# A graph-attention layer on one core: five growing chunks of edges in two shared DRAM tables, instead of four chunks with a table each

## The chip, the cores and the metric

The kernel runs on one core of a Trainium2 chip. The metric is the time of one execution on the device in microseconds; the times before the change come from 16 runs. One execution was also taken with the hardware profiler; durations in this document come from that one. The engines are TensorE (PE, with its weight loads as PEld), VectorE (DVE), ScalarE (ACT), GpSimd (POOL) and SyncE (SP), which here only issues DMAs.

## The reference: what is computed

A graph with 12,500 nodes of 128 features and 412,500 edges of 64 features, sorted by `dst`. With h = relu(layernorm(x)):

```python
q, k, v = h @ Wq + bq, h @ Wk + bk, h @ Wv + bv
eh = edge_features @ We + be
attn_in = concatenate([q[src], k[dst], eh], axis=-1)          # per edge, 3 x 128
hmid = leaky_relu(attn_in @ A1 + b1, 0.2)                      # per edge, 128
scores = leaky_relu(hmid @ A2 + b2, 0.2)                       # per edge, 8 heads
w = softmax(scores.mean(axis=-1), axis=0)                      # over all edges
out = segment_sum(w[:, None] * v[dst], src, num_segments=N)
y = h @ Wn + bn + out
return x + gamma * layernorm(y) + beta
```

The softmax runs over all edges at once, values are gathered at `dst`, and the sum goes to `src`. So the edges come sorted by one end and are needed by the other.

## The kernel before, in words

**Blocks and tiles.** The nodes are padded to 12,544 and split into 98 blocks of 128: node n is in block n mod 98, at place n // 98 (`place1` holds the place plus one). Edges come in 3,224 tiles of 128, eight tiles to a group (`SUPER`), 403 groups.

**Chunks.** `CHUNKS` cuts the groups into four: 86, 121, 121 and 75 groups. For each chunk a table in DRAM, `tabs[c]`, has for each of the 98 blocks room for `ct` tiles of edges: the mean number of a chunk's edges per block plus 3.75 of its roots, rounded up to tiles. That makes 8, 11, 11 and 7 tiles a block. Behind these rows lies a region of `OTHER` tiles for edges that found no room; those are dealt with by a slow loop at the end (`other_edges`), which doesn't run when there are none. A row has 257 numbers (`ROW`): the place, 128 numbers of the part of the hidden layer that comes from `dst` and the edge, and 128 of the value.

**First stage** (`first_stage(c)`): for each tile of edges two matmuls in one PSUM bank (L679 edge features times folded weights, L682 a window of node rows picked by a selection matrix), moved out by ACT (L662 the place, L665 the rest) into `row`, of which there are seven buffers, each for two tiles; then GpSimd scatters each tile of rows to its slots in the table by an indirect DMA (L621).

**Getting ready** (`ready(c)`): `count` makes a histogram of the chunk's edges by block and lane group; `plan` (L397) turns it into starting slots, and into `trips`, the number of turns of `clear_rest`; `place_slots` (L436) works out each edge's slot by matmuls that add up ranks (L459) and comparisons and maxima on DVE (L452, L503).

**Zeroing.** A slot that no edge took must hold numbers, and its place must be 0, since `scores` (L779) tells free slots by place 0 and gives them -1e30. `clear_ends(c)` zeroes the last two tiles (`SPARE`) of each block's room, 98 DMAs of 257 KB a chunk on SP's queue. `clear_rest(c)` zeroes the tiles before these in a loop, if any block has so few edges that it doesn't reach them.

**Second stage** (`second_stage`): for each block of a chunk SP loads its rows (`load`, L699, six buffers), the places are turned (L709), written to DRAM and spread over the partitions (`put_places` L716, `spread_places` L722, both on SP's queue). Tiles go in quads (`QUAD` is 4): `turn` transposes them on PE (L738) and adds the query part by three matmuls (L741), `steep` applies the leaky rectifier (L749 on ACT, L750 on DVE). Then, once for a block and through one PSUM tile `s_ps`: `heads_of` (L758), `add_bias` (L765), `leaky` (L769), `by_slot` (L775), `scores` (L783 to L789), `turn_top` (L792), `top_of_all` (L796), `spread_top` (L799), `exponentials` (L805 to L810). Last, for each tile, weights on DVE (L824) and the product with the values on PE (L833), added to `acc` (L838). A plan (`at(when, ...)`) puts these jobs into steps, two per quad; the single-tile chain through `s_ps` takes five steps, and the products of a block come `LAG` = 11 steps after its first turn.

**Order.** The last loop (L982) runs c from 0 to the number of chunks: stage c has the first stage of chunk c, the second stage of chunk c - 1, the getting ready of chunk c + 1 and its `clear_ends`. `interleave` mixes their steps in proportion, and PE, DVE, ACT and SP keep the order that is written out (`manual_schedule`), so on each of these engines an instruction that waits holds up all behind it. `clear_rest(c)` stands ahead of each stage; also when it makes no turn, SP waits there for DMAs that it issued. Before the loop, the node tables (`nodes`), the first part of `ready(0)` and `clear_ends(0)` run together. After it come `all_sums` and the writing out of the nodes.

Of the kernel before, what the change touches and what calls it, by code (L numbers as in the profile page):

```python
# [10 lines left out]
FP = mybir.dt.float32  # L11
# [5 lines left out]
ALU = mybir.AluOpType  # L17
AX = mybir.AxisListType
# [4 lines left out]
P = 128  # L23
# [6 lines left out]
SUPER = 8  # L30
# [7 lines left out]

SPARE = 2

OTHER = 960

STR = 5

# [2 lines left out]
ROW = 2 * D + 1  # L47
# [2 lines left out]
MAGIC = float(3 << 22)  # L50

NGRP = 5
CHUNKS = (0.213, 0.3, 0.3, 0.187)
BECAUSE = "worked out within these bounds on the chip"


# [46 lines left out]
def kernel(ctx: ExitStack, tc: tile.TileContext, n_edges, x, src, dst, ea, w_nv, w_qt, w_kt,  # L103
# [12 lines left out]
    nc = tc.nc  # L116
    NP = x.shape[0]
    NTN = NP // P
    NT = src.shape[1]
    NG = NT // SUPER  # L120
    NBIN = DIG * DIG
# [3 lines left out]
    chunks = []  # L125
    g0 = 0
    for i, share in enumerate(CHUNKS):
        n = NG - g0 if i == len(CHUNKS) - 1 else max(1, round(NG * share))
# [4 lines left out]
    NC = len(chunks)  # L133
    most_tiles = max(ct for _, _, ct, _ in chunks)

    blocks = []
# [15 lines left out]
    flag_d = dram.tile([P, NT], FP, name="flag_d")  # L152
    hist_d = dram.tile([STR, DIG, DIG], FP, name="hist_d")

    tabs = [dram.tile([(t + min(n * SUPER, OTHER)) * P, ROW], FP, name=f"tab{c}") for c, (_, n, _, t) in enumerate(chunks)]

    late = ctx.enter_context(tc.tile_pool(name="late", bufs=1))
    blank = late.tile([P, SPARE * ROW], FP, name="blank")
# [2 lines left out]
    def clear_ends(c):  # L161

        ct = chunks[c][2]
        k = min(SPARE, ct)
        for b in range(NTN):
            nc.sync.dma_start(out=tabs[c][(b * ct + ct - k) * P:(b + 1) * ct * P, :].rearrange("(p j) r -> p (j r)", p=P),
                             in_=blank[:, 0:k * ROW])
            yield


# [28 lines left out]
    bins_b = const.tile([P, NBIN], BF, name="bins_b")  # L199
    nc.vector.tensor_copy(bins_b, bins_f)  # L200
    edge_f = iota("edge_f", 8 * STR, 0, P, 1)

    part1 = iota("part1", 1, 1, 0, 1)
    third = const.tile([P, 1], FP, name="third")
# [155 lines left out]


    start_of = {}

    def count(c):

# [31 lines left out]
    def plan(c):  # L397

        ct = chunks[c][2]
        whole = ip.tile([1, STR, NBIN], FP, name="whole_h")  # L400
        nc.sync.dma_start(out=whole[:, :STR, :], in_=hist_d.rearrange("s a b -> s (a b)").unsqueeze(0))
        yield
        start_of[c] = ip.tile([1, STR * NBIN], FP, name="start_of")
        so = start_of[c].rearrange("p (s b) -> p s b", s=STR)
        nc.vector.memset(so[:, 0, :], 0.0)
        for s in range(1, STR):
            nc.vector.tensor_add(so[:, s, :], so[:, s - 1, :], whole[:, s - 1, :])

        least = ip.tile([1, 2], FP, name="least")
        total = whole[:, STR - 1, :]  # L410
        nc.vector.tensor_add(total, so[:, STR - 1, :], whole[:, STR - 1, :])

        nc.vector.tensor_reduce(least[:, 1:2], total, AX.X, ALU.max)
        nc.vector.tensor_scalar(least[:, 1:2], least[:, 1:2], MARK, 1e6, op0=ALU.is_ge, op1=ALU.mult)
        nc.vector.tensor_scalar(start_of[c], start_of[c], least[:, 1:2], None, op0=ALU.add)
        nc.vector.tensor_reduce(least[:, 0:1], total[:, 0:NTN], AX.X, ALU.min)
        nc.vector.tensor_scalar(trips[:, c:c + 1], least[:, 0:1], float((ct - min(SPARE, ct)) * P), float(NTN),
                                op0=ALU.is_lt, op1=ALU.mult)
        yield

    def clear_rest(c):

        ct = chunks[c][2]
        rest = ct - min(SPARE, ct)
        if rest > 0:
            turns = nc.values_load(trips[0:1, c:c + 1], min_val=0, max_val=NTN, skip_runtime_bounds_check_because=BECAUSE)
            with tc.For_i(0, turns, 1) as b:
                for j in range(rest):
                    nc.sync.dma_start(out=tabs[c][ds(b * (ct * P) + j * P, P), :], in_=blank[:, 0:ROW])

    def values(row, engine, high):

# [182 lines left out]
    def scatter(c, g, k, row, sent):  # L615

        g0 = chunks[c][0]
        m = min(P, n_edges - (g * SUPER + k) * P)
        if m > 0:
            t = (g - g0) * SUPER + k  # L620
            i = nc.gpsimd.indirect_dma_start(  # L621
                out=tabs[c][:, :], out_offset=bass.IndirectOffsetOnAxis(ap=slots[c][t // (8 * STR)][:m, t % (8 * STR):t % (8 * STR) + 1], axis=0),
                in_=row[:m, :], in_offset=None)

            for other in sent[-OTHER + 1:]:
                tc.declare_no_dep(i.ins, other, reason="every edge has a slot of its own")
            sent.append(i.ins)
# [64 lines left out]
    def second_stage():  # L692
# [6 lines left out]
        def load(i):  # L699
            c, b, ct, _, _ = blocks[i]  # L700
            rows_of[i] = pb.tile([P, most_tiles, ROW], FP, name="rows_of")
            nc.sync.dma_start(out=rows_of[i][:, 0:ct, :],
                              in_=tabs[c][b * ct * P:(b + 1) * ct * P, :].rearrange("(p j) r -> p j r", p=P))
            qws[i] = ps.tile([P, 3 * D], BF, name="qw")
            nc.sync.dma_start(out=qws[i], in_=q_tab[b])

# [71 lines left out]

        def scores(i):  # L779

            _, b, ct, _, _ = blocks[i]
            none = ps.tile([P, most_tiles], FP, name="none")[:, 0:ct]
            nc.vector.tensor_scalar(none, rows_of[i][:, 0:ct, 0:1].rearrange("p j r -> p (j r)"), 0.0, -1e30,  # L783
                                    op0=ALU.is_equal, op1=ALU.mult)
            state["score", i] = score = ps.tile([P, most_tiles + 1], FP, name="score")
            nc.vector.tensor_copy(score[:, ct:ct + 1], most_of[:, b:b + 1])
            nc.vector.tensor_add(score[:, 0:ct], state["s_ps"][:, 0:ct], none)
# [276 lines left out]
```

## Time and profile before

| | |
|---|---|
| median of 16 runs | 6141.63 us (6125.76 to 6165.45) |
| the profiled execution | 6131.44 us, span 6129.7 us |
| busy: PE, DVE, POOL, ACT | 4973.3, 4535.7, 3382.2, 2204.1 us |
| mean granted clock of TensorE | 0.915 |
| moved by DMA | 1362.10 MB, 222 GB/s over the span |
| first scatter; stages 1, 2, 3 begin (first scatter of their chunk); last scatter ends | 470.1; 1404.8, 2724.8, 4136.1; 5220.8 us |
| last addition to `acc` ends | 5987.1 us |

The lines are read like this: a group's line has the source line, engine, operation, what it writes from what, the count, then busy us, mean ns of one, and the idle time just before them with what ended it. Matmuls overlap in these records, so that groups add up to more than the busy time of their engine. A stage is judged by the windows between the times above, not by the shares over the whole span: the first stage of the loop has no attention in it, and the last has no scatter.

### The profile page before, as it was taken

What the parts mean: (1) busy time and instruction counts of PE and PEld (TensorE: products, weight loads), DVE (VectorE), ACT (ScalarE), POOL (GpSimd) and SP (SyncE); (2) the same over time, 40 slices, a digit from 0 to 9 for tenths busy, and PEclk for the clock granted to TensorE, in tenths of its full rate; (3) what the DMA queues carried; (4) which work ended last, traced back from release to release, by engine and by line L of the source; (5) the groups of instructions that cost most, each with busy time, mean ns of one, the idle gap of its engine ahead of it and who ended that gap; (6) DMA issues with size and microseconds to landing.
All of it is one profiled execution on the core that took longest, in us unless ns stands there. A gap on an engine that the chain in (4) does not pass through costs nothing. (4 is left out here: it accounts for less than half of the span.)

```text
span 6129.7 us, 98826 instructions
## 1 busy us (share of the span) xinstructions
PE 4973.3 (81%) x31430; PEld 3421.5 (56%) x31788; DVE 4535.7 (74%) x14001; ACT 2204.1 (36%) x5624; POOL 3382.2 (55%) x3236
## 2 busy tenths in 40 slices
PE   1556676658988999879998989979999999888880
PEld 0223343335666666656666666657777777656550
DVE  4886686657877777768777777767777777777779
ACT  0452222223444444434444444434444444333331
POOL 0007777777777777767777777765555565000000
PEclk9777767778999999989999999989999999999995
DMA  9345555557888888877888988877888878444443
GB/s 202 119 158 176 169 164 171 171 162 244 259 253 261 259 259 262 256 225 257 276 279 274 284 274 271 276 238 255 261 261 264 260 265 258 154 151 150 156 129 126
DMA packets 607897, 1362.10 MB, mean 222 GB/s; under 512 B 120436, under 2 KB 337196, under 8 KB 569352
## 3 DMA queue, kind: packets, MB, share of 16 engines
q1 hardware_dynamic: 423284, 877.57, 48.8%
q0 software_dynamic: 154704, 424.26, 19.3%
q10 hardware_dynamic: 29380, 53.87, 2.6%
q8 instruction: 252, 4.13, 0.3%
q14 instruction: 277, 2.27, 0.1%
HBM read 782.14 MB, written 573.14 MB: 221 GB/s over the span
## 5 line engine op out<-in xcount | busy, mean ns | idle before, releaser
L621 POOL DMA_INDIRECT tab<-row,slots x3223 | 3380.4, 1049 | 1820.3 <-issue 720.1
L679 PE MATMUL row_ps<-w_ea,ea_t 128*128 128x256 f32 x3224 | 1103.3, 427 | 292.5 <-ACT row L665 255.4
L833 PE MATMUL o_ps<-rows_of,w 128*128 128x128 f32 x7252 | 1087.1, 293 | 12.6 <-DVE w L824 11.7
L665 ACT ACTIVATE row<-row_ps 128x512 f32<-128x512 f32 x1612 | 944.2, 586 | 415.9 <-PE row_ps L682 392.8
L824 DVE TENSOR_SCALAR w<-iota_f,rows_of,score 128x128 f32<-128x128 f32 x3626 | 1025.5, 353 | 6.3
L750 DVE TENSOR_TENSOR rows_of<-h_ps,low 128x512 f32<-128x512 f32 (+1 forms) x980 | 634.3, 647 | 469.4 <-ACT low L749 466.3
L679 PEld LDWEIGHTS row_ps<-w_ea,ea_t 128*128 128x128 f32 x3224 | 600.4, 209 | 649.8 <-ACT row L665 430.7
L833 PEld LDWEIGHTS o_ps<-rows_of,w 128*128 128x128 f32 x7252 | 918.7, 196 | 43.0 <-DVE w L824 23.8
L749 ACT ACTIVATE low<-h_ps 128x512 f32<-128x512 f32 (+1 forms) x980 | 552.0, 563 | 860.8 <-PE h_ps L741 856.3
L741 PE MATMUL h_ps<-sel_q,qw 128*128 128x512 bf16 (+1 forms) x2582 | 719.8, 365 | 52.5 <-DVE sel_q L729 32.2
L682 PE MATMUL row_ps<-kv,sel 126*128 126x256 bf16 x3224 | 668.2, 291 | 18.2 <-DMA offs<-off_d 15.7
L662 ACT ACTIVATE row<-place 128x2 f32<-128x2 bf16 x1612 | 318.7, 198 | 997.4 <-DMA tab<-row,slots 971.3
L503 DVE TENSOR_REDUCE num<-run 128x5 f32<-128x500 f32 x646 | 433.3, 671 | 297.5 <-PE run L459 297.3
L738 PE MATMUL h_ps<-ident,rows_of 128*128 128x128 f32 x3626 | 574.0, 278 | 0.0
L775 PEld LDWEIGHTS s_ps<-heads,z 96*128 96x128 f32 (+1 forms) x3136 | 392.7, 194 | 206.2 <-DVE z L769 191.1
L682 PEld LDWEIGHTS <-sel 126*128 126x128 bf16 x3224 | 338.8, 105 | 299.6 <-issue 76.5
L758 PE MATMUL s_ps<-rows_of,a_sb 128*32 128x512 f32 (+1 forms) x1960 | 454.2, 579 | 55.8 <-DVE most_of L805 31.6
L738 PEld LDWEIGHTS h_ps<-ident,rows_of 128*128 128x128 f32 x3626 | 436.1, 144 | 107.9 <-issue 81.7
L775 PE MATMUL s_ps<-heads,z 96*128 96x3 f32 (+1 forms) x3136 | 415.2, 253 | 88.2 <-DVE z L769 87.5
L765 ACT ACTIVATE z<-s_ps,b_col 64x512 f32<-64x512 f32 (+1 forms) x392 | 266.7, 680 | 512.9 <-PE s_ps L758 512.1
L452 DVE TENSOR_TENSOR one<-bins_b,block 128x500 f16<-128x500 bf16 x646 | 431.3, 668 | 1.7 <-PE run L459 1.6
L729 DVE TENSOR_SCALAR sel_q<-pls,part 128x1408 bf16<-128x1408 uint8 (+2 forms) x392 | 333.2, 850 | 116.9 <-DMA pls<-pl_d 107.7
(172 smaller groups left out, 4725.9 us busy)
## 6 DMA issues: line engine op xcount, KB each, us to landing
rows_of<-tab SPq DMA_DIRECT2D x196, 1413.5 KB
ea_t<-in_ea SPq DMA_DIRECT2D x403, 256.0 KB
tab<-blank SPq DMA_DIRECT2D x392, 257.0 KB
rows_of<-tab SPq DMA_DIRECT2D x98, 1028.0 KB
rows_of<-tab SPq DMA_DIRECT2D x98, 899.5 KB
tab<-row,slots POOLq DMA_INDIRECT x3223
offs<-off_d SPq DMA_DIRECT2D x403, 126.0 KB
qw<-q_tab SPq DMA_DIRECT2D x392, 96.0 KB
```

What stands on the lines that cost most here:

```text
L621: i = nc.gpsimd.indirect_dma_start(out=tabs[c][:, :], out_offset=bass.IndirectOffsetOnAxis(ap=slots[c][t // (8 * STR)][:m, t % (8 * STR):t ...
L665: nc.scalar.activation(row[:, :, 1:ROW], bank, AF.Copy)
L679: nc.tensor.matmul(bank[:, :, 0:D], lhsT=ea_g[:, ts(k, P)], rhs=w_ea, start=True, stop=False, skip_group_check=True)
L682: nc.tensor.matmul(bank[:, b, :], lhsT=sel[:, ts(b * halves + k, P)], rhs=kv, start=False, stop=True, skip_group_check=True)
L738: nc.tensor.matmul(h_ps[:, ts(j, P)], lhsT=rows_of[i][:, q * QUAD + j, 1:D + 1], rhs=ident, is_transpose=True, start=j == 0, stop=False, s ...
L741: nc.tensor.matmul(h_ps[:, 0:m * P], lhsT=qws[i][:, ts(k, D)], rhs=plss[i][:, q * QUAD * P:(q * QUAD + m) * P], start=False, stop=k == 2, ...
L749: nc.scalar.activation(low, h_ps, AF.Copy, scale=SLOPE)
L750: nc.vector.tensor_max(rows_of[i][:, q * QUAD:q * QUAD + m, 1:D + 1], h_ps.rearrange("p (j e) -> p j e", j=m), low.rearrange("p (j e) -> p ...
L758: nc.tensor.matmul(state["s_ps"][32 * q:32 * (q + 1), 0:m * P], lhsT=a2_sb, rhs=rows_of[i][:, q * QUAD:q * QUAD + m, 1:D + 1], start=True, ...
L775: nc.tensor.matmul(state["s_ps"][:, 0:nq * QUAD].rearrange("p (q j) -> p j q", j=QUAD)[:, j, :], lhsT=state["z"][:32 * nq, ts(j, P)], rhs= ...
L824: nc.vector.tensor_scalar(w, iota_f, rows_of[i][:, t, 0:1], state["score", i][:, t:t + 1], op0=ALU.is_equal, op1=ALU.mult)
L833: nc.tensor.matmul(state["o_ps"][:, 0:D], lhsT=w, rhs=rows_of[i][:, t, D + 1:ROW], start=t == 0, stop=t == ct - 1)
```

## The change

The edges are cut into five chunks of 50, 62, 86, 109 and 96 groups. Chunk c uses table c mod 2, so that chunks 0, 2 and 4 share one table and 1 and 3 the other. `held[c]` is the number of tiles that earlier chunks filled in the same table; the ends of a chunk's blocks are zeroed only where they lie behind that, and `clear_rest` and its test are limited to those blocks too. Since what lies in a free slot may now be an old edge's row with a place of its own, free slots are no longer told by place 0: `plan` spreads each block's number of edges over the partitions (`taken[c]`), and `scores` compares slot numbers (`slot_of`) with it. `OTHER` goes from 960 to 840.

```diff
-OTHER = 960
+OTHER = 840
-CHUNKS = (0.213, 0.3, 0.3, 0.187)
+CHUNKS = (0.124, 0.154, 0.2135, 0.2705, 0.238)
...
-    tabs = [dram.tile([(t + min(n * SUPER, OTHER)) * P, ROW], FP, name=f"tab{c}") for c, (_, n, _, t) in enumerate(chunks)]
+    tiles_of = [max(t + min(n * SUPER, OTHER) for _, n, _, t in chunks[i::2]) for i in range(2)]
+    tabs = [dram.tile([t * P, ROW], FP, name=f"tab{i}") for i, t in enumerate(tiles_of)]
+
+    held = [max([t for _, _, _, t in chunks[c % 2:c:2]], default=0) for c in range(NC)]
...
         for b in range(NTN):
-            nc.sync.dma_start(out=tabs[c][(b * ct + ct - k) * P:(b + 1) * ct * P, :].rearrange("(p j) r -> p (j r)", p=P),
-                             in_=blank[:, 0:k * ROW])
+            if (b + 1) * ct > held[c]:
+                nc.sync.dma_start(out=tabs[c % 2][(b * ct + ct - k) * P:(b + 1) * ct * P, :]
+                                  .rearrange("(p j) r -> p (j r)", p=P), in_=blank[:, 0:k * ROW])
             yield
...
+    slot_of = {ct: iota(f"slot{ct}", ct, 0, 1, ct) for ct in sorted({ct for _, _, ct, _ in chunks})}
...
-        nc.vector.tensor_reduce(least[:, 0:1], total[:, 0:NTN], AX.X, ALU.min)
-        nc.vector.tensor_scalar(trips[:, c:c + 1], least[:, 0:1], float((ct - min(SPARE, ct)) * P), float(NTN),
+        b0 = min(held[c] // ct, NTN - 1)
+        nc.vector.tensor_reduce(least[:, 0:1], total[:, b0:NTN], AX.X, ALU.min)
+
+        nc.vector.tensor_scalar(total, total, least[:, 1:2], None, op0=ALU.subtract)
+        run = ps_c.tile([P, 512], FP, name="run")
+        nc.tensor.matmul(run[:, 0:NBIN], lhsT=ones[0:1, :], rhs=total, start=True, stop=True)
+        taken[c] = late.tile([P, NBIN], FP, name=f"taken{c}")
+        nc.vector.tensor_copy(taken[c], run[:, 0:NBIN])
+        nc.vector.tensor_scalar(trips[:, c:c + 1], least[:, 0:1], float((ct - min(SPARE, ct)) * P), float(NTN - b0),
                                 op0=ALU.is_lt, op1=ALU.mult)
...
-        if rest > 0:
-            turns = nc.values_load(trips[0:1, c:c + 1], min_val=0, max_val=NTN, skip_runtime_bounds_check_because=BECAUSE)
+        b0 = held[c] // ct
+        if rest > 0 and b0 < NTN:
+            turns = nc.values_load(trips[0:1, c:c + 1], min_val=0, max_val=NTN - b0, skip_runtime_bounds_check_because=BECAUSE)
             with tc.For_i(0, turns, 1) as b:
                 for j in range(rest):
-                    nc.sync.dma_start(out=tabs[c][ds(b * (ct * P) + j * P, P), :], in_=blank[:, 0:ROW])
+                    nc.sync.dma_start(out=tabs[c % 2][ds(b * (ct * P) + (b0 * ct + j) * P, P), :], in_=blank[:, 0:ROW])
...
         def scores(i):
 
-            _, b, ct, _, _ = blocks[i]
+            c, b, ct, _, _ = blocks[i]
             none = ps.tile([P, most_tiles], FP, name="none")[:, 0:ct]
-            nc.vector.tensor_scalar(none, rows_of[i][:, 0:ct, 0:1].rearrange("p j r -> p (j r)"), 0.0, -1e30,
-                                    op0=ALU.is_equal, op1=ALU.mult)
+            nc.vector.tensor_scalar(none, slot_of[ct], taken[c][:, b:b + 1], -1e30, op0=ALU.is_ge, op1=ALU.mult)
```

The scatter and the loads of the second stage take `tabs[c % 2]` for `tabs[c]`; all else is as before. In both kernels every block's edges fit its room, and every block fills all but its last two tiles: neither `clear_rest` nor `other_edges` makes a turn on this input.

## The prediction

> **What bounds the kernel now.** I read first the page's 40 slices, then the busy time by stage (windows cut where the scatter of a new chunk starts), then the waits of the stage in which one half of the work stands alone, and last the windows around a stage's start. "Stage k" is the pass of the last loop in which chunk k is built; the chunk before it is consumed in the same stage.
>
> The page: busy tenths of TensorE, VectorE and GpSimd, then the granted clock.
>
> ```profile
> span 6129.7 us, 98826 instructions
> PE   1556676658988999879998989979999999888880
> ...
> DVE  4886686657877777768777777767777777777779
> ...
> POOL 0007777777777777767777777765555565000000
> PEclk9777767778999999989999999989999999999995
> ```
>
> TensorE is full from slice 10 on, but not before: there GpSimd alone is steady, and in the last slices GpSimd has nothing left. By stage (columns: window, its length, then busy us of PE, weight loads, DVE, ACT, POOL with instruction counts, clock, DMA share, GB/s):
>
> ```profile
> 470.00:1405.00 935.00, 631.81 (x3092) 348.06 (x3091) 607.87 (x1690) 240.98 (x697) 711.66 (x689) 0.76 0.52 168
> 1405.00:2725.00 1320.00, 1166.45 (x7421) 814.87 (x7525) 997.03 (x3215) 531.08 (x1437) 999.21 (x969) 0.94 0.84 256
> 2725.00:4136.00 1411.00, 1275.74 (x8532) 934.72 (x8637) 1052.99 (x3325) 578.88 (x1554) 1026.14 (x968) 0.96 0.85 269
> 4136.00:5222.00 1086.00, 1043.05 (x7030) 772.70 (x7127) 816.12 (x2644) 453.37 (x1191) 643.41 (x599) 1.00 0.80 259
> 5222.00:5987.00 765.00, 668.82 (x4294) 458.04 (x4343) 588.96 (x2130) 233.65 (x500) 0.00 (x0) 1.00 0.45 147
> 5987.00:6130.00 143.00, 0.59 (x2) 0.50 (x2) 134.89 (x223) 19.95 (x41) 0.00 (x0) 0.51 0.41 135
> ```
>
> Stage 0 and stage 1 are GpSimd's: the timeline shows each scatter busy 0.96 to 1.5 us and then 0.30 us of issue, and 935 us / 688 is 1.359 us a scatter; in stage 1, 1307 us / 968 is 1.351. The page has the scatter as its dearest row:
>
> ```profile
> L621 POOL DMA_INDIRECT tab<-row,slots x3223 | 3380.4, 1049 | 1820.3 <-issue 720.1
> ```
>
> In stage 2 GpSimd and TensorE are both nearly full and neither is quite; stage 3 is TensorE's (1043 of 1086 us). In stage 4 attention runs alone, 7.47 us a block, and TensorE waits in it for one chain through one PSUM tile (the waits of PE in that stage: total us, times, longest):
>
> ```profile
> PE s_ps L799 <- DVE top_of L796: 58.0, 94, 0.7
> PE s_ps L775 <- DVE z L769: 26.7, 94, 1.5
> ```
>
> That is 0.9 us a block: heads, bias, leaky, turn, maximum, spread follow one another through PE, ACT and DVE, whatever number of tiles the block has.
>
> **What the work costs.** From the instruction records I took how far each instruction moves the end of its engine's work on (its end less the latest end before it). In stage 3, at full clock, PE needs for one attention tile two products of 129 ns, a turn of 110 and three query matmuls per quad of 224 (183 a tile): 0.551 us; for one block heads 1.12, eight L775 of 0.120, two L799 of 0.154, L709 0.22, L792 0.12: 2.73 us whatever its tiles; for one tile built 0.218 + 0.111 = 0.329 us. Placing costs PE 0.119 us a tile (two L459 of 228 ns per five, L389 28). DVE, likewise: tile 0.513, block 2.12, built tile 0.085, placing with counting 0.353. These give PE 1133, 1251, 1058 and 646 us in stages 1 to 4, where the windows say 1166, 1276 (at clocks of 0.94 and 0.96), 1043 and 669; and DVE 1034, 1055, 812, 560 against 997, 1053, 816, 589. So they may be used.
>
> **The change, part by part.**
>
> The chunks. Tiles a block go from 8, 11, 11, 7 to 5, 6, 8, 10, 9 (37 to 38, from the mean plus 3.75 roots in the code), quads from 10 to 12, blocks from 392 to 490. That adds 98 tiles and 98 blocks: 98 x (0.551 + 2.73) = 322 us of PE and 98 x (0.513 + 2.12) = 258 us of DVE. The work that stood alone at the start shrinks: 400 scatters for 688, at 1.359 us 543 us for 935, **-392 us**. With it 288 built tiles (95 us of PE) and the placing of 760 tiles (90 us of PE, 268 of DVE) move into the mixed stages. Demands of the new stages, in us:
>
> - stage 1 (62 groups, blocks of 5, placing 688): PE 783, DVE 744, POOL 672 (496 x 1.355)
> - stage 2 (86, blocks of 6, placing 872): PE 922, DVE 875, POOL 932
> - stage 3 (109, blocks of 8, placing 768): PE 1077, DVE 955, POOL 1182
> - stage 4 (96, blocks of 10): PE 1060, DVE 775, POOL 1039
> - stage 5 (blocks of 9 alone): PE 754, DVE 660
>
> What a stage takes over its largest demand is read from before, starts of stages included: 1.01 where one engine leads clearly (stage 1: 1320 over 1308, PE at 0.87 of it); 1.079 where two are level (stage 2: 1411 over 1308, PE at 0.96); 1.027 where PE leads and POOL is at 0.77 (stage 3: 1086 over 1058); 1.184 where attention is alone in two quads (stage 4: 765 over 646). So the new stages, with both ends from these rows:
> - Stage 1 has PE and DVE at 0.95 of each other and the two-quad chain: between 1.01 and 1.184, nearest to a mix of the last and the level case; 1.12, **877 us** (791 to 927).
> - Stage 2 has three engines within 6%: 1.027 to 1.184; a little over the level case, 1.09, **1016** (957 to 1103).
> - Stage 3, PE at 0.91 of POOL, half-way between 0.87 and 0.96: 1.035, **1223** (1194 to 1275).
> - Stage 4 is the level case without placing: 1.07, **1134** (1089 to 1144).
> - Stage 5: 754 plus 0.9 us x 98 of the chain's waits plus the 23 us of filling and draining that stage 4 of before has over its blocks (765 less 98 x 7.47, with rounding ahead): **865** (777 with all waits hidden behind the third quad, 893 at 1.184).
> Their sum is 5115 us for 4582, **+533 us**.
>
> Preparing. Only the steps up to the first slots lie ahead of the first scatter (470 us in). Counting chunk 0 takes 16 steps for 28; a step is 1.56 us of DVE, which is busy 212 of the 240 us to 440. 12 x 1.56 x 0.9: **-17 us** (0 if the offsets from DRAM end it, as its last wait says; -25 with PE's part).
>
> Edges counted per block. In each plan a subtraction on DVE, a matmul with one row of weights and a copy from PSUM, through the bank that counting and placing use too. PE stands in order behind the subtraction, and the placing of that chunk behind the copy. Nearest rows: L415 0.47 us on 1x500, L799 0.15, L838 0.35 from PSUM: about 1.2 us x 5, **+6** (0 where a scatter backlog covers it, 10 if each engine waits twice). Five more iotas run on an idle GpSimd, their copies cost DVE 1 us. The comparison per block reads a row of slots for the place column: L783 moves DVE's end by 120 ns either way, so nothing.
>
> Clearing. 284 DMAs of 257 KB for 392. SP gives each 0.36 us; GpSimd, not DMA, set the rate in stage 1 at a DMA share of 0.84 and also in stage 0 at 0.52. So nothing; with the cover gone it could give 108 x 0.36 = 39 us of SP. Against it, 98 more blocks issue four DMAs each (0.34 + 0.45 + 0.36 + 0.32 us: 144 us of SP).
>
> Two tables. A new chunk's scatters must follow the last loads of the chunk two before. SP waits for its DMAs at every stage's start already (before the first loads of the new chunk, and behind it stand all of that stage's loads; PE, then ACT and POOL wait for those). Windows around the start of stage 2:
>
> ```profile
> 2711.00:2715.00 4.00, 0.00 (x0) 0.00 (x0) 0.00 (x0) 0.28 (x2) 1.05 (x2) 0.90 0.18 66
> 2715.00:2719.00 4.00, 0.00 (x0) 0.00 (x0) 0.00 (x0) 0.00 (x0) 0.00 (x0) 0.50 0.97 360
> 2719.00:2723.00 4.00, 1.19 (x2) 0.50 (x2) 0.48 (x1) 0.00 (x0) 0.00 (x0) 0.50 0.98 285
> ...
> 2727.00:2731.00 4.00, 4.00 (x25) 2.25 (x24) 3.39 (x14) 1.66 (x5) 1.22 (x3) 0.89 0.45 132
> ```
>
> About 10 us of PE idle, and half clock until about 2728. This start comes once more than before, and it lies inside the ratios above.
>
> A rule to weigh against that row: the Trainium skill ("TensorE: Matmul & The Clock Gate", Part 1) says that an idle window of about 3.4 us halves the clock and about 3.4 us of sustained work restores it. The row agrees: 0.50 after the gap, 0.89 some 8 us later. By the page alone one more start would cost about 2 us beyond its idle time, an estimate (half of 3.4 us lost); by the row, which is slow for about 8 us, about 4.
>
> **Sum.** +533 - 392 - 17 + 7 = +131 us on the profiled execution's 6131 us, 10 us under the median of 6142: **6260 us**.
>
> **The rivals.**
> - *Faster: the mixed stages pack as well as the best two of before.* More placing and building between the chain's steps fills PE's waits. For it: stage 3 of before, 96% busy. Against: DVE was at 0.77 of PE there and is at 0.95 in the new stages 1 and 2. Ratios of 1.027, 1.04, 1.01, 1.027 and 842 for stage 5 (754 and the chain's 88, nothing else) give 804 + 969 + 1194 + 1089 + 842 = 4898: 6045 us. It decides from a sum of 4984, a mean ratio of 1.058 (before: 4582 over 4320, 1.061; I forecast 1.086).
> - *Slower still: the chain bounds small blocks.* In stages 1 and 2 PE and DVE serve each other in turns, and placing stands in both queues. At 1.184 (927 and 1103) the sum is 6400. For it, the 0.9 us above; against it, that it was measured with nothing to fill the gaps.
> - *SP.* The spread of the places waits on SP for its own earlier write: 511.5 us in 94 times in stage 1 of before, 5.4 us a block, longest 10.0. A new stage-1 block has 8.9 us; issues 2.5 + 5.4 = 7.9. With waits of 8 us it is 10.5 x 98 = 1029: 6412 us.
> - *Nothing comes of it:* what stage 0 gives is what the extra blocks take, 6130 to 6155.
>
> **How the numbers follow.** Forecast 0.58, the faster rival 0.21, the chain 0.11, SP 0.05, a tie 0.05. About 0.2% is what a measurement of this kernel can tell from no change: faster 0.21, same 0.05, slower 0.74. The range takes in half of the faster rival and the chain, 6070 to 6400; the forecast alone is 6180 to 6340.
>
> **What would show it.** First scatter at about 453 us; stage 0 about 543 us at 1.36 us a scatter; in stage 1 PE under 92% busy with POOL clearly under its 1.35 us rhythm (1.75 or more a scatter); stage 3 at 1.40; a last stage of 8.6 us a block; PE's busy time up by some 320 us. Wrong if stage 1 takes under 820 us or stage 2 under 960, if a block's fixed 2.73 us of PE isn't paid again, or if edges overflow a block and the loop over other edges runs.

## The result and the profile after

The changed kernel takes 6442.43 us (median of 8 runs, 6420.51 to 6447.54) where the kernel before takes 6141.73 us: a ratio of 1.0485, 95% interval 1.0472 to 1.0498. It is slower by some 300 us, where 118 more than the median before were forecast; it lies 42 us above the upper end of the forecast range, 6400. The profiled execution took 6414.59 us, its span 6412.9; it is 28 us under the median, so the table below shows that much less of the miss.

The page of the changed kernel, the rows that were shown of before:

```profile
span 6412.9 us, 106611 instructions
PE   2557659888889999998999999899999998888880
...
POOL 0037764555556777776777777677777740000000
...
L636 POOL DMA_INDIRECT tab<-row,slots x3223 | 3360.9, 1043 | 1855.0 <-issue 712.1
L847 PE MATMUL o_ps<-rows_of,w 128*128 128x128 f32 x7448 | 1192.3, 300 | 145.6 <-DVE w L838 139.4
```

GpSimd starts earlier and stops earlier, and TensorE fills up from slice 7, where it was slice 10. What is new is the last row: the products wait 139 us for their weights, where before the same row (L833) waited 11.7. The windows by stage say where (window, length, then busy us of PE, weight loads, DVE, ACT, POOL with counts, clock, DMA share, GB/s):

```profile
411.60:955.00 543.40, 348.70 (x1648) 195.69 (x1647) 314.57 (x872) 137.41 (x400) 406.92 (x401) 0.74 0.59 189
955.00:1901.90 946.90, 824.55 (x5370) 552.08 (x5449) 743.91 (x2620) 349.33 (x975) 518.27 (x496) 0.94 0.68 198
1901.90:2921.50 1019.60, 941.44 (x6402) 662.18 (x6497) 875.70 (x2988) 433.55 (x1177) 725.64 (x689) 0.98 0.80 233
2921.50:4127.20 1205.70, 1108.49 (x7209) 786.27 (x7314) 957.57 (x3117) 511.73 (x1363) 905.25 (x873) 0.96 0.80 246
4127.20:5236.30 1109.10, 1044.25 (x6998) 775.49 (x7096) 796.11 (x2538) 485.82 (x1351) 804.83 (x767) 0.99 0.84 269
5236.30:6269.40 1033.10, 866.73 (x5375) 589.71 (x5475) 707.27 (x2446) 251.97 (x605) 0.02 (x1) 0.91 0.42 137
```

| us | forecast | measured | difference |
|---|---|---|---|
| ahead of the first scatter | 453 | 411.6 | -41 |
| stage 0 | 543 | 543.4 | 0 |
| stage 1 | 877 | 946.9 | +70 |
| stage 2 | 1016 | 1019.6 | +4 |
| stage 3 | 1223 | 1205.7 | -17 |
| stage 4 | 1134 | 1109.1 | -25 |
| stage 5 | 865 | 1033.1 | +168 |
| writing out | 143 | 143.5 | 0 |

The forecast's miss lies in three rows: stage 5, stage 1, and a gain ahead of the first scatter that was larger than thought. In the last stage the granted clock is 0.91, where the last stage of before had 1.00.

The last stage close up: a part of the timeline of one block of nine tiles (start, length, engine, line, operation, in brackets the idle time before it and what ended it). In the rows of L847 `x2` is the product of one tile and `x8` that of four.

```profile
5702.26 0.49 PE L847 MATMUL o_ps<-rows_of,w 128*128 128x128 f32 x2
...
5702.58 0.27 PE L753 MATMUL h_ps<-ident,rows_of 128*128 128x128 f32 x1
...
5702.69 0.69 DVE L765 TENSOR_TENSOR rows_of<-h_ps,low 128x512 f32<-128x512 f32 x1 [1.43 <-ACT low L764]
5702.69 0.33 PE L756 MATMUL h_ps<-sel_q,qw 128*128 128x128 bf16 x3
...
5703.67 0.30 ACT L824 ACTIVATE score<-score,shift_of 128x10 f32<-128x10 f32 x1 [1.01 <-DVE shift_of L822]
...
5704.01 1.11 DVE L838 TENSOR_SCALAR w<-iota_f,rows_of,score 128x128 f32<-128x128 f32 x4
...
5704.41 1.26 PE L847 MATMUL o_ps<-rows_of,w 128*128 128x128 f32 x8 [1.38 <-DVE w L838]
```

The third quad has one tile. Its turn and its product occupy TensorE for well under 1 us, and then TensorE has nothing left in its order but the products of the next block's first quad, whose weights DVE (L838) makes only after the rectifier of a full quad (L765) and the exponentials (L824). TensorE waits 1.38 us here, and about as long in every block. Its waits in 95 blocks of the stage (5290 to 6260 us; total us, times, longest):

```profile
PE o_ps L847 <- DVE w L838: 131.2, 95, 1.4
PE s_ps L790 <- DVE z L784: 16.4, 68, 0.3
```

### The profile page after: what moved, and what is told of

Read it like the earlier page. It is cut to its first block, busy times and chain, and to the rows that moved or that the text cites. A ratio compares the mean times of both kernels' runs of the same rounds, so it can differ in the third digit from the quotient of the medians.

```text
span 6412.9 us, 106611 instructions
## 1 busy us (share of the span) xinstructions
PE 5316.4 (83%) x33771; PEld 3646.9 (57%) x34251; DVE 4855.8 (76%) x15501; ACT 2335.0 (36%) x6114; POOL 3363.1 (52%) x3241
## 5 line engine op out<-in xcount | busy, mean ns | idle before, releaser
L847 PE MATMUL o_ps<-rows_of,w 128*128 128x128 f32 x7448 | 1192.3, 300 | 145.6 <-DVE w L838 139.4
L838 DVE TENSOR_SCALAR w<-iota_f,rows_of,score 128x128 f32<-128x128 f32 x3724 | 1070.9, 352 | 25.8 <-issue 11.0
L765 DVE TENSOR_TENSOR rows_of<-h_ps,low 128x512 f32<-128x512 f32 (+2 forms) x1176 | 674.9, 574 | 532.4 <-ACT low L764 528.6
L847 PEld LDWEIGHTS o_ps<-rows_of,w 128*128 128x128 f32 x7448 | 973.2, 199 | 180.5 <-DVE w L838 160.7
L764 ACT ACTIVATE low<-h_ps 128x512 f32<-128x512 f32 (+2 forms) x1176 | 592.7, 504 | 996.7 <-PE h_ps L756 973.7
L756 PE MATMUL h_ps<-sel_q,qw 128*128 128x512 bf16 (+2 forms) x3048 | 757.9, 330 | 52.0 <-DVE sel_q L744 27.0
L773 PE MATMUL s_ps<-rows_of,a_sb 128*32 128x512 f32 (+2 forms) x2352 | 584.6, 573 | 52.4 <-DVE most_of L819 38.9
L790 PEld LDWEIGHTS s_ps<-heads,z 64*128 64x128 f32 (+1 forms) x3920 | 478.4, 191 | 242.9 <-DVE z L784 185.6
L790 PE MATMUL s_ps<-heads,z 64*128 64x2 f32 (+1 forms) x3920 | 517.9, 253 | 86.3 <-DVE z L784 84.8
L780 ACT ACTIVATE z<-s_ps,b_col 64x512 f32<-64x512 f32 (+1 forms) x490 | 334.1, 682 | 663.6 <-PE s_ps L773 658.3
L784 DVE SCALAR_TENSOR_TENSOR z<-z 64x512 f32<-64x512 f32 (+1 forms) x490 | 334.6, 683 | 199.4 <-ACT z L780 196.1
L744 DVE TENSOR_SCALAR sel_q<-pls,part 128x640 bf16<-128x640 uint8 (+4 forms) x490 | 364.4, 744 | 134.6 <-DMA pls<-pl_d 134.2
```

Of the source, the lines that this page charges most:

```text
L756: nc.tensor.matmul(h_ps[:, 0:m * P], lhsT=qws[i][:, ts(k, D)], rhs=plss[i][:, q * QUAD * P:(q * QUAD + m) * P], start=False, stop=k == 2, ...
L764: nc.scalar.activation(low, h_ps, AF.Copy, scale=SLOPE)
L765: nc.vector.tensor_max(rows_of[i][:, q * QUAD:q * QUAD + m, 1:D + 1], h_ps.rearrange("p (j e) -> p j e", j=m), low.rearrange("p (j e) -> p ...
L773: nc.tensor.matmul(state["s_ps"][32 * q:32 * (q + 1), 0:m * P], lhsT=a2_sb, rhs=rows_of[i][:, q * QUAD:q * QUAD + m, 1:D + 1], start=True, ...
L790: nc.tensor.matmul(state["s_ps"][:, 0:nq * QUAD].rearrange("p (q j) -> p j q", j=QUAD)[:, j, :], lhsT=state["z"][:32 * nq, ts(j, P)], rhs= ...
L838: nc.vector.tensor_scalar(w, iota_f, rows_of[i][:, t, 0:1], state["score", i][:, t:t + 1], op0=ALU.is_equal, op1=ALU.mult)
```

## The experiments

They ran in four groups, each on a chip of its own with the kernel before beside it; the kernel before took 6147.67 us beside the runs from own tables to blocks nine apart, 6213.57 beside those from four growing chunks to blocks eight apart, 6842.06 beside the three that follow and 6209.31 beside the last two. So ratios to it are what is compared.

**The chunks alone.** The kernel before with the new shares and the smaller `OTHER`; each chunk has its own table, and all ends are zeroed, as before:

```diff
-OTHER = 960
-CHUNKS = (0.213, 0.3, 0.3, 0.187)
+OTHER = 840
+CHUNKS = (0.124, 0.154, 0.2135, 0.2705, 0.238)
```

> The kernel before with the five new chunks alone: each chunk keeps a table of its own, all 490 block ends are zeroed, free slots are told by place 0. If the chunks alone make the kernel slower, this takes what the changed kernel takes, 6400 to 6450 us, with a last stage of 1033 us and a stage 1 of about 947. If sharing tables, the edge counts per block or the waits for old loads cost, it comes out clearly lower, down to the 6260 that I had forecast from the chunks' work.

Measured: 6470.49 us, ratio 1.0529 (1.0509 to 1.0549). The chunks alone account for all of the loss, and for a little more: the rest of the change gives back some 0.44%, about 27 us. Its stages, in the same columns as above:

```profile
957.50:1904.90 947.40, 829.30 (x5450) 553.35 (x5450) 738.85 (x2619) 349.78 (x975) 520.51 (x497) 0.94 0.75 214
1904.90:2957.60 1052.70, 966.02 (x6506) 671.31 (x6503) 872.85 (x2992) 434.20 (x1180) 726.16 (x688) 0.96 0.82 240
2957.60:4188.30 1230.70, 1123.61 (x7302) 794.99 (x7301) 950.58 (x3108) 513.30 (x1361) 906.81 (x872) 0.94 0.85 260
```

Stage 1 and the last (1037.4 us) are as in the changed kernel; stage 2 is 33 us longer and stage 3 25 us. In these two it zeroes 98 ends each, where the changed kernel zeroes 40 and 11; in stage 1 it is 98 for 37, and the length is the same, with the DMA engines at 0.75 and not at 0.82 and 0.85. That the zeroing is what makes the two longer fits these lines, but shared tables, edge counts and zeroing were not tried apart.

**Even quads.** A block's tiles are dealt evenly to its quads, with no work taken away:

```diff
+        def wide(i):
+            return _ceil(blocks[i][2], blocks[i][3])
...
-            m = min(QUAD, blocks[i][2] - q * QUAD)
+            W = wide(i)
+            m = min(W, blocks[i][2] - q * W)
...
             for j in range(QUAD):
-                nc.tensor.matmul(state["s_ps"][:, 0:nq * QUAD].rearrange("p (q j) -> p j q", j=QUAD)[:, j, :],
+                to = (state["s_ps"][:, 0:nq * W].rearrange("p (q j) -> p j q", j=W)[:, j, :] if j < W
+                      else state["s_ps"][:, nq * j:nq * (j + 1)])
+                nc.tensor.matmul(to,
...
```

(the other uses of `q * QUAD` become `q * W`)

> The changed kernel with a block's tiles dealt evenly to its quads: 5 as 3+2 (was 4+1), 6 as 3+3 (was 4+2), 9 as 3+3+3 (was 4+4+1); 8 and 10 stay. The eight by_slot matmuls a block are kept, so no work goes. Theory of the short quad: a quad of one tile gives TensorE about 0.35 us to do while it should cover a chain step of 1.1 to 1.4 us; then the last stage falls from 1033 to about 840 us, stage 1 from 947 to about 880, stage 2 by up to 20, and the kernel to about 6165 (6130 to 6220). Theory of the fixed cost per block (98 more blocks at 2.73 us of TensorE): nothing but the last digits moves, 6400 to 6450.

Measured: 6234.02 us, ratio 1.0149 (1.0130 to 1.0168), so 3.4% of the time of before comes back, some 208 us. The windows of its stages 1 and 5, and TensorE's waits in its last stage (total us, times, longest):

```profile
960.30:1863.50 903.20, 799.06 (x5441) 560.46 (x5441) 743.42 (x2620) 349.30 (x974) 519.16 (x496) 0.94 0.72 207
...
5216.90:6087.50 870.60, 802.45 (x5477) 566.17 (x5475) 698.52 (x2446) 263.64 (x605) 0.00 (x0) 1.00 0.51 163
```

```profile
PE s_ps L799 <- DVE z L790: 45.2, 95, 1.5
PE o_ps L857 <- DVE w L848: 15.1, 95, 0.2
```

The last stage falls from 1033 to 871 us, the wait for weights from 131.2 to 15.1 us (the one on `z` grows from 16.4 to 45.2), and the clock is 1.00. Stage 1 falls by 44 us; stage 2 doesn't (1030.3 for 1019.6), though its blocks of 6 went from 4+2 to 3+3. A quad of two tiles was cover enough. The total came out 70 us above the 6165 that was expected, and above its range (6130 to 6220): 903 for 880 in stage 1, 871 for 840 in the last.

**TensorE kept busy.** Nothing is evened out; matmuls that nobody reads fill the wait of the last stage:

```diff
             if q == 0:
                 state["o_ps"] = ps_o.tile([P, 512], FP, name="o_ps")
+                if blocks[i][0] == NC - 1:
+                    for k in range(4):
+                        nc.tensor.matmul(t_bank[:, 2 * P:3 * P], lhsT=ident, rhs=ident, start=True, stop=True,
+                                         skip_group_check=True)
```

> The changed kernel with four more 128x128 float32 matmuls per block of the last chunk, into an unused part of a PSUM bank that nobody reads, just ahead of the products that wait 1.4 us for their weights in the last stage. Theory that these waits drop the granted clock (0.91 in the last stage, blocks of 9.42 and 10.85 us by turns): the clock goes to 1.00 and every block takes about 9.42 to 9.5, so some 65 us less, 6370 to 6385. Rival, that the clock falls for another reason and TensorE is the limit: about 1.1 us more for each of 98 blocks, 6480 to 6550.

Measured: 6364.25 us, ratio 1.0362 (1.0339 to 1.0386): added work made the kernel faster. Its last stage:

```profile
5255.70:6214.90 959.20, 885.88 (x6262) 655.39 (x6260) 706.82 (x2446) 252.01 (x605) 0.02 (x1) 1.00 0.47 148
```

The clock is 1.00 and a block takes 9.38 us (10.15 on average in the changed kernel, whose blocks take either 9.42 or 10.9). The blocks are as long as the faster ones of the changed kernel, so the added matmuls cost nothing here, and of the last stage's 1033 us 74 were the slow clock, and the next 88 (959 to 871) are the short quad itself, as the run with even quads shows.

**Blocks nine tiles apart**, in the kernel before: an unused tile after each block of chunk 0's table.

```diff
-        chunks.append((g0, n, tiles, NTN * tiles))
+        step_of.append(tiles + (i == 0))
+        chunks.append((g0, n, tiles, NTN * step_of[i]))
...
```

(`step_of[c]` takes the place of `ct` where a block's first row in the table is worked out)

> The kernel before with one change: the blocks of chunk 0's table lie nine tiles apart for eight (an unused tile between them; 1,184,256 bytes for 1,052,672). Theory that the zeroing of chunk 0's block ends is slow before the change (154 us for 98 DMAs, 98 us in the changed kernel) because successive ends lie just over 2^20 bytes apart: zeroing takes about 100 us, the first scatter comes at about 430 us for 470, and the kernel takes 35 to 50 us less, about 6095. Rival, that it depends on something else (which steps stand between the DMAs, the size of the tables): first scatter at 465 to 475, the time of the kernel before.

Measured: 6098.63 us, ratio 0.9922 (0.9902 to 0.9941), the first scatter at 428.0 us. The first 150 us of the kernel before, and of this run:

```profile
0.00:50.00 50.00, 3.64 (x12) 2.78 (x12) 24.68 (x44) 1.28 (x1) 1.75 (x13) 1.00 0.98 216
50.00:100.00 50.00, 7.02 (x109) 4.30 (x110) 36.79 (x54) 0.21 (x1) 0.00 (x0) 1.00 1.00 231
100.00:150.00 50.00, 5.47 (x117) 4.08 (x113) 7.47 (x44) 0.00 (x0) 0.00 (x0) 1.00 0.99 162
```

```profile
0.00:50.00 50.00, 3.64 (x12) 2.78 (x12) 24.68 (x44) 1.28 (x1) 1.75 (x13) 1.00 0.97 273
50.00:100.00 50.00, 7.22 (x111) 4.50 (x112) 36.79 (x54) 0.20 (x1) 0.00 (x0) 1.00 0.98 301
100.00:150.00 50.00, 29.39 (x472) 19.85 (x472) 41.60 (x176) 9.74 (x15) 0.00 (x0) 1.00 0.40 107
```

In the first 100 us the core's DMAs, mostly the same ones, run at 273 and 301 GB/s for 216 and 231 (last column), with the DMA engines full in both, and from 100 us on TensorE and VectorE have work. The kernel takes 49 us less, as expected.

**Four growing chunks**, each with its own table, in even quads; a quad's fourth `by_slot` step is left out where quads have three tiles:

```diff
-CHUNKS = (0.213, 0.3, 0.3, 0.187)
+CHUNKS = (0.186, 0.273, 0.3, 0.241)
...
-            for j in range(QUAD):
+            for j in range(W):
...
```

> The kernel before, each chunk with its own table, but four chunks that grow at the start: 75, 110, 121, 97 groups (7, 10, 11, 9 tiles a block, 37 in all as before, 392 blocks as before), tiles dealt evenly to the quads. Theory that the start alone was worth shrinking and the added 98 blocks were what cost: stage 0 takes 600 x 1.359 = 815 us (935 before), stage 1 about 1200, stage 2 about 1335, stage 3 about 1185, the last stage about 870 (765 before): 5405 us for 5517, and about 40 us less ahead of the first scatter since the blocks of chunk 0 lie 921,312 bytes apart: 5975 us (5930 to 6030). Rival, that any shift of work out of stage 0 is given back in the mixed stages: 6090 to 6150.

Measured: 6066.38 us, ratio 0.9762 (0.9746 to 0.9778): faster than both kernels. Stages: 813, 1234, 1409, 1182 and 854 us, against 815, 1200, 1335, 1185 and 870 expected. Stage 2 misses most, by 74 us: with 968 scatters beside blocks of 10 tiles it takes as long as stage 2 of before (1411) with blocks of 11. As a ratio the total is inside what was expected (5930 to 6030 over 6142 is 0.966 to 0.982).

**One step less a block.** The even quads with three `by_slot` steps for four where quads have three tiles (the diff's second half above).

> The run with even quads, with three by_slot steps for four where quads have three tiles (blocks of 5, 6 and 9: chunks 0, 1 and 4): two TensorE instructions of 120 ns less in each of 294 blocks, 71 us of TensorE. It prices what a block costs on TensorE whatever its tiles. If that fixed cost is on the path of the small-block stages, 45 to 70 us go (6165 to 6190), a third each from stages 1, 2 and 5. If the chain's latencies or VectorE set these stages, under 20 us.

Measured: 6261.44 us, ratio 1.0086 (1.0063 to 1.0109) on a chip that is slower for the kernel before, against 1.0149 on the other: about 39 us, between the two cases. A block of the last stage takes 8.28 us for 8.49, nearly the whole 0.24 us of the two instructions. They are part of the chain through the scores, so this doesn't tell TensorE's time from the chain's: that stays open. This run and the four growing chunks were measured on one chip, both with even quads and the shorter `by_slot`: five chunks take 6261 us there, four 6066. Stage 0 is 266 us shorter with five (547 for 813), the stages behind it together 454 longer (5134 for 4680). So the fifth chunk with its 98 blocks costs more than it gains, also without short quads. (The five have the shared tables too; by the run with the chunks alone these cost nothing on balance.)

**Blocks eight tiles apart, with five chunks**: the run with the chunks alone, but chunk 0's blocks of five tiles at the old distance.

```diff
+        step_of.append(8 if i == 0 else tiles)
```

> The run with five chunks and own tables, but chunk 0's blocks of five tiles laid eight tiles apart, 1,052,672 bytes as in the kernel before. It is the counterpart of the run that laid the kernel before nine apart. If the distance near 2^20 bytes is what makes the zeroing slow, the first 98 DMAs take about 150 us again for 100, the first scatter comes at 450 to 470 us for 410, and the kernel takes 35 to 50 us more than its sister, 6505 to 6520. If the number of tiles or the order of steps matters, nothing changes: 6460 to 6480.

Measured: 6620.67 us, ratio 1.0650 (1.0630 to 1.0670) against 1.0529 for its sister: some 74 us more, where 35 to 50 were expected. Its first 150 us:

```profile
0.00:50.00 50.00, 3.63 (x12) 2.78 (x12) 22.13 (x43) 1.28 (x1) 1.75 (x13) 1.00 1.00 200
50.00:100.00 50.00, 3.66 (x23) 1.49 (x24) 35.56 (x37) 0.21 (x1) 0.00 (x0) 1.00 1.08 223
100.00:150.00 50.00, 5.05 (x116) 3.87 (x112) 6.56 (x35) 0.00 (x0) 0.00 (x0) 1.00 1.00 167
```

The slow zeroing is back, and the first scatter comes at 474.3 us for 410.3. The two sisters ran on different chips, so the 64 us, and the 74, may hold a share of the chip.

**Four growing chunks as cut before**, the last chunk's blocks of nine in 4+4+1: the kernel before with the shares alone.

```diff
-CHUNKS = (0.213, 0.3, 0.3, 0.187)
+CHUNKS = (0.186, 0.273, 0.3, 0.241)
```

> The run with four growing chunks (75, 110, 121, 97 groups), but with the quads as the kernel before cuts them: the last chunk's blocks of nine are 4+4+1 again. The other chunks' quads are as in that run but for nothing (7 is 4+3, 10 is 4+4+2, 11 is 4+4+3 in both). If the short quad is what spoils a last stage of nines, that stage takes about 1030 us for 854, with blocks of 9.4 and 10.9 us and a clock near 0.91, and the kernel is about 2.8% slower than that run, ratio to the kernel before about 1.005. If the last stage was long in the changed kernel for a reason that comes with the five chunks or the shared tables, the ratio stays at 0.976 to 0.985.

Measured: 7033.4 us, ratio 1.0287 (1.0262 to 1.0312), on a chip where the scatters come slower (1.52 to 1.55 us each in stage 0 of the three kernels run there, 1.36 to 1.38 elsewhere) and the ratios of before don't carry over. So the total says nothing about the expected 1.005. The last stage has no scatters; the run with even quads takes 8.50 us a block in it there and 8.49 elsewhere, so it can be compared:

```profile
5846.50:6888.50 1042.00, 878.06 (x5404) 596.59 (x5502) 704.46 (x2458) 252.65 (x605) 0.01 (x1) 0.90 0.45 136
```

1042 us at a clock of 0.90, where even quads took 871, and 854 with the shorter `by_slot`: the short quad and nothing of the five chunks or the tables makes this stage long.

**TensorE loaded.** Even quads, and the four matmuls that nobody reads in all 490 blocks:

```diff
+                for k in range(4):
+                    nc.tensor.matmul(t_bank[:, 2 * P:3 * P], lhsT=ident, rhs=ident, start=True, stop=True,
+                                     skip_group_check=True)
```

> The run with even quads, with four 128x128 float32 matmuls that nobody reads added to each of the 490 blocks, ahead of the block's first products: about 1.05 us of TensorE a block, 515 us in all, not in the chain through the scores. It prices TensorE time added per block. If TensorE is the bound where scatters don't lead, nearly all of it shows in stages 1, 2, 4 and 5 and half in stage 3: 300 to 460 us more than its sister, 6530 to 6690. If waits on VectorE and the chain set these stages, the matmuls fill the waits and under 150 us come on top, as in the last stage of the run that kept TensorE busy, where they cost nothing.

> The run with even quads once more, as the sister of the run before it on the same chip: ratio 1.01 to 1.02 to the kernel before.

Measured: 7123.76 us for 7063.19 of the sister (ratios 1.0412 and 1.0321), both on the slow chip: 61 us for 515 us of TensorE work. The sister's own ratio missed its expected 1.01 to 1.02 there. Stage 1 and the last stage, first of the sister, then of this run:

```profile
1037.00:2010.60 973.60, 831.74 (x5441) 577.14 (x5440) 744.90 (x2620) 346.70 (x974) 520.60 (x496) 0.91 0.66 192
6081.60:6954.10 872.50, 804.69 (x5476) 568.54 (x5476) 698.52 (x2446) 263.19 (x605) 0.00 (x0) 1.00 0.52 162
...
1037.10:2008.30 971.20, 877.80 (x6185) 642.43 (x6184) 746.68 (x2620) 348.43 (x974) 517.11 (x497) 0.95 0.68 193
6124.40:7007.60 883.20, 828.84 (x6299) 647.10 (x6299) 699.42 (x2451) 263.14 (x605) 0.02 (x1) 1.00 0.51 161
```

In the last stage, the one that compares with the other chips, 103 us of added work cost 10.7 (883.2 for 872.5); in stage 1 as much cost nothing, though there the clock rose from 0.91 to 0.95 with it, which may hide a part. So time added to TensorE at this place in the order hardly lengthens the last stage, though TensorE was busy for 805 of its 872 us. What does set its length is not shown: TensorE's recorded waits in the sister's last stage are 58 us, and 9 of them went, so most of the added work found room in time that the records count as busy. In the mixed stages this chip left more waits to fill than the first one, and what TensorE time costs there on the first chip stays open.

**Growing against the distance alone**, on one chip.

Two edits shown above, unchanged: the blocks nine apart in the kernel before, and the four growing chunks in even quads.

> The kernel before with chunk 0's blocks nine tiles apart once more, as the sister of the next run on one chip: ratio to the kernel before 0.985 to 0.994. It holds only the faster zeroing.

> The run with four growing chunks and even quads once more, beside the run that only lays the blocks apart. Both zero fast (blocks 921,312 and 1,184,256 bytes apart). If shrinking the scatter-only stage pays by itself, this is clearly below its sister: 0.975 to 0.982 to the kernel before, 60 to 120 us less than the sister. If all of its gain was the zeroing, the two are within 20 us of each other.

Measured: 6154.55 us, ratio 0.9909 (0.9883 to 0.9935), and 6058.58 us, ratio 0.9751 (0.9727 to 0.9774): 96 us apart. Four growing chunks in even quads pay beyond the faster zeroing. Some 20 of the 96 us may be the shorter `by_slot` of the last stage (850 us for 871 in the run with one step less).

## Why the prediction was wrong

The direction was right, and the start gains 392 us as forecast (543 us). The five stages behind it take 5314 us where the four of before took 4582: 732 more, with 533 more forecast. Stages 2, 3 and 4 came within 2.5%: the ratios of a stage to its largest demand carried there. That the added blocks take more than the start gains holds also without short quads (the two runs on one chip, five chunks against four). With even quads the loss is 1.5%, some 90 us, where 118 were forecast; the short quads are the rest.

What a block costs is less sure than the sum made it. Its main term is TensorE's time, and this didn't bound stage 5 of the run with even quads: 103 us more of it, at one place in the order, cost 10.7 us on the slow chip (and nothing in stage 1, at a higher clock). And that TensorE's busy time rose by 343 us (about 320 forecast) is partly luck: with even quads, the same work, it rises by 259, and 64 of the other 84 lie in the last stage with its slow clock.

**Stage 5** was the step that failed: 754 us of demand plus the chain's 0.9 us a block plus filling, 865, with the remark that a third quad might hide the chain's waits. The two waits that the 0.9 us stand for did shrink: the one on the maximum, 58.0 us before, is gone, and the one on `z` is 16.4 us for 26.7. But a third quad of one tile gives TensorE too little to do, and a wait came out that the sum did not have, 1.38 us a block on the weights; the clock fell with it. Of the 168 us missed, 88 are the short quad at full clock (959 us with TensorE kept busy, 871 with even quads, where the wait on the weights is 116 us less and that on `z` 29 more), 74 are the clock (1033 for 959), and 6 remain. The quads were there to count (9 is 4+4+1), but I took a block's stall from a kernel whose blocks of seven are 4+3. That only 6 us remain is luck: with even quads TensorE is busy 802 us of the stage and idle 68, where the sum had 754 and 111 (in stage 4 of before the records had 669 us for 646 by the same working, so only a part of the 48 is in how busy time is counted).

**Two slips in the sum.** The filling and draining of stage 4 of before, 765 less 98 x 7.47, is 33 us and not 23. And 131 us on the profiled 6131 are 6262; the 10 us up to the median were not added.

**Stage 1**: 1.12 of the largest demand, 877 us, with an end at 927; it took 947. The 44 us that even quads give back are again the quad of one tile (5 is 4+1); the other 26 stay unexplained. TensorE's longest waits in this stage name the chain, first in the changed kernel, then with even quads:

```profile
PE s_ps L813 <- DVE top_of L810: 68.8, 66, 3.6
...
PE s_ps L822 <- DVE top_of L819: 29.4, 41, 2.7
```

With even quads the stage is 903, inside the ends. The rival "the chain bounds small blocks" had this stage in kind, but it had stage 2 too, which came as forecast, and not the last stage, which missed most. That its total, 6400, came nearer than the forecast is luck, and so it is with SP's 6412.

**Preparing**: -17 us forecast, -58.5 measured. I counted steps on VectorE and passed over its longest wait before the change, 42.6 us for the zeroing:

```profile
DVE off_t L337 <- DMA tab<-blank: 42.6, 1, 42.6
```

That zeroing got faster because chunk 0's blocks moved from 1,052,672 to 657,920 bytes apart; the runs at nine and at eight tiles show it in both directions (-42 us, +64 us). What is left of the 58.5, some 16, is close to the 17 forecast.

**Clearing** was costed at nothing since GpSimd sets the rate. The run with the chunks alone is 0.44% slower than the changed kernel, and longer in two stages in which it zeroes more while the DMA engines are above 0.8, so the fewer DMAs may be worth some 27 us; this is argued, not shown. It also leaves nothing on balance for the edge counts (+6 forecast) and the waits for old loads.

**The other rivals.** SP's waits didn't decide: in stage 1 SP waited 331.9 us in 87 times for the places, 3.8 us each (5.4 before), a block's time was 9.7 us for the 10.5 that this rival had, and of TensorE's waits there only one, 8.0 us for edge features, ends with a DMA. The tie fell with the size of the loss. The faster rival's point, a mean ratio of 1.058, was not met: the five stages' sum is 5314 us over 4711, 1.128, and with even quads 903 + 1030 + 1203 + 1120 + 871 = 5127 us, 1.088, about what I had forecast (1.086) without thinking of the short quads.

## What to carry to other kernels

When a change alters how work is cut into pieces, count the remainders: a remainder piece with little to do takes the cover from the waits beside it, and a chain that was hidden by full pieces comes out once per block. Shrinking a stage in which only one engine works was worth it here as long as the number of blocks stayed and no piece was left short: four growing chunks in even quads gained 2.4% (0.8 to 0.9 of it by faster zeroing), five in even quads lost 1.5%, and five with short quads 4.9%. And the price of a stage's stall belongs to its shape; it shouldn't be taken over to another shape without walking through the order once.

## What was unexpected in the hardware

**The clock can fall after a window that is 60% busy.** In the changed kernel's last stage the granted clock drops to 0.50 for 3.41 us, 51 times between 5300 and 6230 us, though TensorE never waits longer than 1.4 us. Windows of 3.41 us around two drops (the first figure after the length is TensorE's busy time, the clock is third from the end):

```profile
5690.31:5693.72 3.41, 2.03 (x15) 1.29 (x12) 1.82 (x8) 1.06 (x3) 0.00 (x0) 1.00 0.84 275
5693.72:5697.13 3.41, 3.41 (x14) 1.55 (x13) 2.70 (x10) 0.00 (x0) 0.00 (x0) 0.50 0.30 118
5697.13:5700.55 3.42, 3.12 (x24) 2.52 (x24) 1.96 (x7) 1.43 (x3) 0.00 (x0) 1.00 0.02 3
5700.55:5703.96 3.41, 2.47 (x19) 1.69 (x17) 1.65 (x6) 0.89 (x3) 0.00 (x0) 1.00 0.82 196
...
5710.79:5714.20 3.41, 2.03 (x15) 1.34 (x13) 1.94 (x8) 1.06 (x3) 0.00 (x0) 1.00 0.87 308
5714.20:5717.61 3.41, 3.41 (x15) 1.53 (x14) 2.58 (x10) 0.00 (x1) 0.00 (x0) 0.50 0.21 80
```

Each of the 51 drops follows a window in which TensorE was 59 or 60% busy (2.03 of 3.41 us). 33 windows between 61 and 80% were not followed by one, and seven at 59 or 60% weren't either, so the share of busy time in these records doesn't decide alone. In the last stage of the kernel before, between 5250 and 5950 us, such windows were at least 82% busy, and there was no drop; nor was there one with TensorE kept busy (87% and more) or with even quads (84% and more). The Trainium skill ("TensorE: Matmul & The Clock Gate", Part 1) has the length of the window, 3413 ns, an idle window as what throttles, and the rule "no PE-idle gaps >~3.4µs"; it also tells of one kernel whose clock swung under short but frequent idling. This trace agrees with the latter, and the rule alone would have missed it: short waits within one window are enough here, and the measurement decides.

**Zeroing targets 1,052,672 bytes apart are slow.** With this distance (2^20 + 4,096 bytes) from one DMA's target to the next, the core's DMA moved 162 to 231 GB/s while the 98 DMAs of 257 KB ran; with 657,920, 921,312 or 1,184,256 bytes it was 257 to 318. The Trainium skill ("DMA: Bandwidth & Descriptors", Latency and other measured facts) knows slow row pitches at large powers of two within one DMA, put right by 4 KiB more. Here the distance is between successive DMAs, and 4 KiB over the power of two is the slow case. Whether the nearness to 2^20 is the reason was not tried: only one such distance was.

**Chips differ.** On one chip the kernel before took 6842 us, for 6142 to 6214 on the others. In stage 0 of the run with even quads a scatter is busy as long there as elsewhere (1021 for 1029 ns), but scatters come every 1.55 us for 1.37. GpSimd's waits for rows account for it, first on the slow chip, then on the other (total us, times, longest):

```profile
POOL tab L636 <- ACT row L677: 87.8, 36, 11.6
...
POOL tab L636 <- ACT row L677: 6.4, 18, 1.2
```

The last stage, without scatters, took the same as elsewhere (872.5 for 870.6 us). What makes the rows late on that chip stays open.
